# Projections that load weights for two pairs, x in four resting buffers, and causal pairs made ahead in pinned steps

## The chip, the cores and the metric

The kernel runs on one core of one Trainium2 chip. The core has a matmul engine (TensorE, PE), whose weight loads the profile lists as PEld, an elementwise engine (VectorE, DVE), an activation engine (ScalarE, ACT), GpSimd (POOL) and an engine that here only issues DMAs (SyncE, SP). Each works through its own queue in order. The metric is device time in microseconds (us) of one execution, the median of the runs; lower is better.

## The reference

The input x has the shape (4, 512, 128, 64): four batches, 512 time steps, and D = 128 x 64 = 8192 features. All is float32. Layer 0 does, for each batch:

```
xn = layernorm(x)                                  # over D
k, v, r = xn @ Wk, xn @ Wv, sigmoid(xn @ Wr)       # D -> 64
s[t] = decay * s[t-1] + k[t] * v[t]
x = x + (r * s) @ Wo                               # 64 -> D
x = x + gelu(conv3 over the 128 (layernorm(x)))    # 64 -> 64 channels
to = depthwise causal conv of 3 taps over time (layernorm(x))
x = x + layernorm(to)
x = x + gelu(x @ W1 + b1) @ W2 + b2                # 64 -> 256 -> 64
```

Layer 1 takes a moving average over 25 steps as the trend, sends the rest through a Fourier transform over time, mixes 128 modes with complex weights for each of the 64 channels, transforms back and adds the trend. The change touches layer 0 only.

## The kernel before

Layer 0 keeps features on the 128 partitions and time on the free axis: D is 64 chunks of 128, handled as 32 pairs of chunks (`NPR`), a tile of 128 x 2 x 512 values each. Each batch goes through these stages, which are Python generators:

- J, `project` (L321): for each pair it loads weights (L337, 256 KB), the transposed x (`load_x`, L293, 512 KB) and the same part of x with tokens on the partitions (`xk`, L340, 512 KB). DVE takes statistics of `xk` (L344) and scales the weights in place (L357); PE multiplies (L360). `xk` serves the statistics and nothing else.
- Z, `scan` (L371): the recurrence over time.
- A, `attend_and_convolve` (L466): the output of the attention, then the convolution over frequency. It uses the tags x1, z, x2 and sq; its result goes to DRAM as `x2d`.
- C, `convolve_time` (L581): the causal convolution over time. For a pair, `taps` (L553) loads `x2d` (L555), normalizes in two DVE operations (L556, L557), scales on ACT for each half j of the pair (L560), adds two taps per half on DVE (L564), corrects the first two time steps on POOL (L568) and stores to `tod` (L569, from POOL's queue).
- O, `open_feed` (L639), and F, `feed_forward` (L647): 64 steps c and two that drain. A step widens chunk c (`widen`, L656, into the banks m and c, gelu on ACT at L660), prepares the residual of a later pair (`residual`, L619, in even steps: loads at L549, DVE at L624 and L625; `add_residual`, L628, in odd steps: ACT at L633, DVE at L636), narrows chunk c - 1 (`narrow`, L662: PE at L667 into the single bank p, DVE empties it into x4t at L672) and transposes and stores chunk c - 2 (`store`, L675, L681 to L692).

Two stages of different batches run side by side. `in_turn` (L726) steps whichever of the two is behind by its share; this fixes the order in which instructions are traced. PE keeps that order exactly (`manual_schedule`). On the other engines, DMA queues included, a planner orders the instructions: it runs a model of the program, and whenever an engine is free in that model it takes, of the instructions whose data and buffers are ready, the one traced first. So work traced late can go early. `tc.keep_in_program_order(ins)` takes from an instruction the freedom to go ahead of the instruction traced just before it on its engine.

Around the change, F of batch 0 runs beside J and Z of batch 2, and F of batch 1 beside J and Z of batch 3. In these two stages F also works ahead: `convolve_ahead` (L571) builds the two rows that scale batch b + 1 (`rows`, L279: `spread` at L240 writes the bank p, ACT copies it at L284) and then makes `AHEAD` = 12 of the 32 pairs of the causal convolution of batch b + 1, in tiles x1 (three buffers) and z (four). `feed_forward` calls it at the head of every fourth step:

```
        for c in range(NCH + 2):
            if b + 2 < B and c % 4 == 3:
                early = early or convolve_ahead(b + 1)
                next(early, None)
```

Steps 3 and 7 make the rows, steps 11, 15, ... 55 a pair each.

In J of batches 1, 2 and 3 (once a scan is done) weights and `xk` of a pair share one tile of the tag wx, which has two buffers:

```
                both = spare("wx", 4 * S + SL)
                wq, xk = both[:, :, 0 : 4 * S], both[:, :, 4 * S :]
```

Of the kernel before, what the change touches and what calls it, by code (L numbers as in the profile page):

```python
# [12 lines left out]
ALU = mybir.AluOpType  # L13
# [9 lines left out]
SL = 512  # L23
# [3 lines left out]
S = 64  # L27
# [52 lines left out]
def layer0(ctx, tc, dram, x, xt, vecs, wkvr, wo, wdec, wconv, fbias, w1, fb1, w2, fb2, x4):  # L80
# [4 lines left out]
    nc = tc.nc  # L85
    B = x.shape[0]
# [7 lines left out]
    bk = ctx.enter_context(tc.tile_pool(name="bk", bufs=2))  # L94
# [8 lines left out]
    def two(pool, tag):  # L103
        return pool.tile([P, 2, SL], F32, tag=tag, name=tag)
# [183 lines left out]
    def pair_of(row):  # L288
        return row.unsqueeze(1).to_broadcast([P, 2, SL])

    def load_x(b, i):
        xp = fr.tile([P, 2, SL], F32, tag="xp", name="xp")
        nc.sync.dma_start(xp, xt[b, 2 * i : 2 * i + 2].rearrange("c p t -> p c t"))  # L293
        return xp

    def spare(tag, n):
        return fr.tile([P, 2, n], F32, tag=tag, name=tag, bufs={"z": 4, "wx": 2}.get(tag, 3))
# [23 lines left out]
    def project(b):  # L321
        pa = two(ps_m, "m") if b == 1 else two(ps_a, "a")
        held[0] = b == 1
        if b == 0:
            psum_w = ps_p.tile([P, SL], F32, tag="p", name="psum_w")
        stt = rowp.tile([P, NT, NS, 6], F32, tag="stt", name="stt")
        for i in range(NPR):
            first, last = i == 0, i == NPR - 1
            if unscanned[0]:

                wq, xk = two(fr, "x1")[:, :, 0 : 4 * S + 3], spare("z", SL)
            else:

                both = spare("wx", 4 * S + SL)
                wq, xk = both[:, :, 0 : 4 * S], both[:, :, 4 * S :]
            n = 4 * S + 2 * (b == 0)
            nc.sync.dma_start(wq[:, :, 0 : n], wkvr[2 * i : 2 * i + 2, :, 0 : n].rearrange("c p s -> p c s"))  # L337
            xp = load_x(b, i)
            s, h = i // 2, i % 2 * 2
            nc.sync.dma_start(  # L340
                xk, x[b, h * P : (h + 2) * P, s * SL : (s + 1) * SL].rearrange("(t p) d -> p t d", p=P)
            )
            for t in range(2):
                nc.vector.bn_stats(stt[:, h + t, s, :], xk[:, t, :])  # L344
            if b == 0:
                nc.gpsimd.memset(wq[:, :, n:], 1.0)
                for j in range(2):
                    c = 2 * i + j

                    w = wq[:, j, :]  # L350
                    nc.tensor.matmul(
                        psum_w[0 : S + 2, 0 : 4 * S + 3], lhsT=w[:, 3 * S : 4 * S + 2], rhs=w,
                        start=c == 0, stop=c == NCH - 1,
                    )
            for j in range(2):
                w = wq[:, j, 0 : 3 * S]
                nc.vector.tensor_scalar_mul(w, w, vec[:, G1, 2 * i + j : 2 * i + j + 1])  # L357
            for j in range(2):
                for k in range(2):
                    nc.tensor.matmul(  # L360
                        pa[:, k, :], lhsT=wq[:, j, k * P : (k + 1) * P], rhs=xp[:, j, :],
                        start=first and j == 0, stop=last and j == 1,
                    )
                yield 1.0
        kvrg = rowp.tile([P, 2, SL], F32, tag="kvrg", name="kvrg")
        nc.scalar.copy(kvrg, pa)
        held[0] = False
        projected[b] = (kvrg, stt, psum_w) if b == 0 else (kvrg, stt)
# [181 lines left out]
        return t  # L550


    def taps(b, i, x2, xr, to, rb, mb):  # L553

        nc.sync.dma_start(x2, x2d[b][2 * i : 2 * i + 2].rearrange("c p t -> p c t"))  # L555
        nc.vector.tensor_tensor(xr, x2, pair_of(rb), ALU.mult)  # L556
        nc.vector.tensor_tensor(xr, xr, pair_of(mb), ALU.subtract)  # L557
        for j in range(2):
            c = slice(2 * i + j, 2 * i + j + 1)
            nc.scalar.activation(  # L560
                to[:, j, :], xr[:, j, :], AF.Identity, bias=tb_all[:, c], scale=vec[:, W2, c]
            )
            for k, w in ((1, W1), (2, W0)):
                nc.vector.scalar_tensor_tensor(  # L564
                    to[:, j, k:], xr[:, j, : SL - k], vec[:, w, c], to[:, j, k:], ALU.mult, ALU.add
                )
        cc = slice(2 * i, 2 * i + 2)
        nc.gpsimd.tensor_tensor(to[:, :, 0:2], to[:, :, 0:2], fix[:, cc, :], ALU.add)  # L568
        nc.gpsimd.dma_start(tod[b][cc].rearrange("c p t -> p c t"), to)  # L569

    def convolve_ahead(b):  # L571


        rb, mb = yield from rows(of_p, *carried[b], "rm3")
        ahead[b] = rb, mb
        for i in range(AHEAD):
            xr = spare("x1", SL)
            taps(b, i, xr, xr, spare("z", SL), rb, mb)
            yield

    def convolve_time(b):  # L581
        bank = of_a if b == B - 1 else of_p
        made = AHEAD if b in ahead else 0
        moment = carried.pop(b)
        if made:
            rb, mb = ahead.pop(b)
        else:
            rb, mb = yield from rows(bank, *moment, "rm" if b == B - 1 else "rm3")
        st = bank()
        waiting, added = [], 0  # L590
        n = NPR - made
        for k in range(n + 2):
            while waiting and waiting[0][0] == k - 2:
                add_up(st, 0, *waiting.pop(0)[1:], added == 0, added == NPR - 1)
                added += 1
            if k < n:
                if b == B - 1:

                    x2, xr, to, sq = spare("xp", SL), spare("x1", SL), spare("z", SL), two(bk, "sq")
                else:  # L600
                    x2 = bk.tile([P, 2, SL], F32, tag="kx", name="x2", bufs=3)
                    xr, to = two(bk, "kd"), bk.tile([P, 2, SL], F32, tag="k3", name="to", bufs=3)
                    sq = bk.tile([P, 2, SL], F32, tag="sq4", name="sq4", bufs=2)
                taps(b, made + k, x2, xr, to, rb, mb)
                nc.scalar.activation(sq, to, AF.Square)
                waiting.append((k, to, sq))
                i = k * made // n
                if i != (k + 1) * made // n:

                    to = fetch("kh", tod, b, i)  # L610
                    sq = bk.tile([P, 2, SL], F32, tag="mid", name="sq5", bufs=4)
                    nc.scalar.activation(sq, to, AF.Square)
                    waiting.append((k, to, sq))
            yield 7.0 * (NPR + 2) / (n + 2)
        mean, sq = yield from finish(st, bank, 4)
        causal[b] = moments(mean, sq, 4)
# [30 lines left out]
    def feed_forward(b):  # L647
# [28 lines left out]
        def store(c):  # L676
            x4t = x4s.pop(c)
            pool, tag = (ps_s, "s") if free_s[0] else (ps_p, "p")
            pt = pool.tile([P, NT, P], F32, tag=tag, name="pt")
            for t in range(NT):  # L680
                nc.tensor.transpose(pt[:, t, :], x4t[:, t * P : (t + 1) * P], ident)  # L681
            s = c // 4
            if c % 4 == 0:
                obs[s] = bk.tile([P, NT, SL], F32, tag="ob", name="ob")
            o = obs[s][:, :, c % 4 * P : (c % 4 + 1) * P]
            if c // 2 % 2:
                for h in range(2):
                    nc.scalar.copy(o[:, :, halves[1 - h]], pt[:, :, halves[h]])
            else:
                nc.scalar.copy(o, pt)  # L690
            if c % 4 == 3:
                nc.gpsimd.dma_start(  # L692
                    x4[b][:, s * SL : (s + 1) * SL].rearrange("(t p) d -> p t d", p=P), obs.pop(s)
                )

        early = None
        for c in range(NCH + 2):
            if b + 2 < B and c % 4 == 3:
                early = early or convolve_ahead(b + 1)
                next(early, None)  # L700
            if c < NCH:
                widen(c, 0)
                widen(c, 1)
            i = c // 2 + 2
            if i < NPR:
                if c % 2:
                    x3s[i] = add_residual(b, i, *coming)
                else:
                    coming = residual(b, i)
            if 0 < c <= NCH:  # L710
                narrow(c - 1)
            if c > 1:
                store(c - 2)
            yield 4.5


# [358 lines left out]
```

## Time and profile before

| | us |
|---|---|
| median of 3 runs | 3857.62 (3856.37 to 3858.19) |
| the profiled execution | 3842.84, its span 3840.8 |
| PE busy | 3619.7, 94% of the span |
| DVE busy | 2692.2, 70% |
| ACT busy | 1764.0, 46% |
| POOL busy | 504.2, 13% |
| DVE waiting for weights at L357 | 167.6 in 59 waits |
| DVE waiting for x at L344 | 92.8 in 60 waits |

A line of the timeline gives the start, the duration, the engine, the source line, the operation with its output and inputs, a count where neighbours are merged, and in square brackets the idle time ahead of it and what ended that. A tile is named by its tag, so "x" stands for several. Matmuls overlap, so their durations do not add up; one float32 matmul of the source appears as two instructions. In a table by stretches each engine has its busy time and, in brackets, its count of instructions; PEclk is the granted share of TensorE's clock.

The steps of F of batch 0 begin at about 822 us and those of F of batch 1 at about 1520 us.

### The profile page before, as it was taken

What the parts mean: (1) busy time and instruction counts of PE and PEld (TensorE: products, weight loads), DVE (VectorE), ACT (ScalarE), POOL (GpSimd) and SP (SyncE); (2) the same over time, 40 slices, a digit from 0 to 9 for tenths busy, and PEclk for the clock granted to TensorE, in tenths of its full rate; (3) what the DMA queues carried; (4) which work ended last, traced back from release to release, by engine and by line L of the source; (5) the groups of instructions that cost most, each with busy time, mean ns of one, the idle gap of its engine ahead of it and who ended that gap; (6) DMA issues with size and microseconds to landing.
All of it is one profiled execution on the core that took longest, in us unless ns stands there. A gap on an engine that the chain in (4) does not pass through costs nothing. (4 is left out here: it accounts for less than half of the span.)

```text
span 3840.8 us, 44890 instructions
## 1 busy us (share of the span) xinstructions
PE 3619.7 (94%) x15945; PEld 1342.6 (35%) x15945; DVE 2692.2 (70%) x3498; ACT 1764.0 (46%) x2491; POOL 504.2 (13%) x782
## 2 busy tenths in 40 slices
PE   9999999988999999899999989999989999999999
PEld 4433322233333223333322323333322753327533
DVE  4455669968656896865689799855559267893577
ACT  0023345645556564555656578867744210142100
POOL 0000012212000121110022121100012100121001
PEclk9999999999999999999999999999999999999999
DMA  9867657777765788777568677645559468994687
GB/s 312 273 216 244 222 195 253 257 246 272 256 227 185 234 276 265 252 255 235 193 232 277 215 243 260 219 154 175 186 190 284 141 212 293 306 311 160 197 292 269
DMA packets 428599, 910.71 MB, mean 237 GB/s; under 512 B 33688, under 2 KB 84056, under 8 KB 424280
## 3 DMA queue, kind: packets, MB, share of 16 engines
q1 hardware_dynamic: 350080, 634.55, 50.3%
q0 software_dynamic: 75776, 271.62, 20.1%
q8 instruction: 127, 2.08, 0.2%
q10 hardware_dynamic: 2520, 1.67, 0.2%
q14 instruction: 96, 0.79, 0.1%
HBM read 639.21 MB, written 268.50 MB: 236 GB/s over the span
## 5 line engine op out<-in xcount | busy, mean ns | idle before, releaser
L667 PE MATMUL pa<-mid,w_sb 128*64 128x512 f32 x2048 | 503.7, 613 | 70.1 <-DVE x4t L672 69.9
L660 ACT ACTIVATE mid<-m,fb_sb 128x1024 f32<-128x1024 f32 x256 | 284.7, 1112 | 243.4 <-PE m L656 243.0
L672 DVE SCALAR_TENSOR_TENSOR x4t<-pa,fb_sb,x 128x512 f32<-128x512 f32 x252 | 187.6, 745 | 208.2 <-PE pa L667 208.2
L656 PE MATMUL m<-x,w_sb 64*128 64x512 f32 x1008 | 291.6, 651 | 1.0 <-ACT mid L660 0.7
L660 ACT ACTIVATE mid<-c,fb_sb 128x1024 f32<-128x1024 f32 x256 | 283.2, 1106 | 1.6 <-PE c L656 1.6
L667 PEld LDWEIGHTS pa<-mid,w_sb 128*64 128x64 f32 x2048 | 125.8, 137 | 417.5 <-issue 221.1
L656 PE MATMUL c<-x,w_sb 64*128 64x512 f32 x1008 | 265.6, 600 | 5.0 <-ACT mid L660 4.9
L360 PE MATMUL a<-xp,wx 128*128 128x512 f32 x512 | 245.0, 605 | 6.2 <-DVE wx L357 5.5
L943 PE MATMUL b<-xin,avg_sb 128*128 128x512 f32 x512 | 230.8, 593 | 3.1 <-DVE xin L949 3.1
L920 ACT COPY two<-a 128x512 f32<-128x512 f32 x64 | 37.5, 586 | 423.9 <-PE a L915 423.9
L523 ACT ACTIVATE sq<-x 128x1024 f32<-128x1024 f32 x128 | 135.0, 1054 | 203.0 <-DVE x L520 203.0
L949 DVE TENSOR_TENSOR xin<-b,pm 128x512 f32<-128x512 f32 x256 | 159.0, 683 | 95.5 <-PE b L946 80.5
L564 DVE SCALAR_TENSOR_TENSOR to<-kd,vec,to 128x510 f32<-128x510 f32 (+1 forms) x288 | 210.5, 743 | 17.9 <-ACT to L560 16.2
L633 ACT ACTIVATE kd<-kd,vec 128x512 f32<-128x512 f32 x256 | 193.5, 809 | 7.2 <-DVE kd L625 7.2
L250 PE MATMUL st<-x,ones 128*32 128x512 f32 x512 | 174.3, 603 | 14.0 <-DVE x L520 13.8
L825 DVE COPY xf<-b 128x256 f32<-128x256 f32 x128 | 54.3, 424 | 188.4 <-PE b L889 187.8
L681 PEld LDWEIGHTS pt<-ident,x4t 128*128 128x128 f32 x1024 | 107.9, 141 | 210.3 <-ACT mid L660 155.0
L846 DVE TENSOR_TENSOR uv<-xin 128x1024 f32<-128x1024 f32 x128 | 155.2, 1228 | 35.2 <-DMA edge<-x 14.7
L344 DVE BATCH_NORM_STATS2 stt<-wx 128x6 f32<-128x512 f32 x174 | 113.0, 685 | 93.3 <-DMA wx<-in_x 92.8
L357 DVE TENSOR_SCALAR wx<-wx,vec 128x192 f32<-128x192 f32 x174 | 48.6, 316 | 184.7 <-DMA wx<-in_wkvr 167.6
L482 PE MATMUL a<-rst,wo_sb 64*128 64x512 f32 x512 | 147.6, 650 | 32.3 <-DVE x L484 30.0
L484 DVE TENSOR_TENSOR x<-a,xp 128x1024 f32<-128x1024 f32 x128 | 156.0, 1219 | 20.9 <-PE a L482 17.6
(239 smaller groups left out, 6649.0 us busy)
## 6 DMA issues: line engine op xcount, KB each, us to landing
xp<-in_xt SPq DMA_DIRECT2D x256, 512.0 KB
xin<-x SPq DMA_DIRECT2D x128, 1024.0 KB
kh<-to SPq DMA_DIRECT2D x152, 512.0 KB
x<-x POOLq DMA_DIRECT2D x128, 512.0 KB, 4.1
kx<-x SPq DMA_DIRECT2D x128, 512.0 KB
x<-ob POOLq DMA_DIRECT2D x64, 1024.0 KB, 6.6
out<-xin POOLq DMA_DIRECT2D x64, 1024.0 KB, 7.3
x<-x SPq DMA_DIRECT2D x96, 512.0 KB
```

Of the source, the lines that this page charges most:

```text
L250: nc.tensor.matmul(st[32 * q : 32 * q + 32, :], lhsT=ones, rhs=src[:, j, :], start=first, stop=last,)
L360: nc.tensor.matmul(pa[:, k, :], lhsT=wq[:, j, k * P : (k + 1) * P], rhs=xp[:, j, :], start=first and j == 0, stop=last and j == 1,)
L484: nc.vector.tensor_tensor(x1, at, xp, ALU.add)
L564: nc.vector.scalar_tensor_tensor(to[:, j, k:], xr[:, j, : SL - k], vec[:, w, c], to[:, j, k:], ALU.mult, ALU.add)
L633: tc.keep_in_program_order(nc.scalar.activation(d[:, j, :], d[:, j, :], AF.Identity, bias=vec[:, B4, c], scale=vec[:, G4, c]))
L656: nc.tensor.matmul(pm[:, h, :], lhsT=w1_sb[hs, m * P : (m + 1) * P], rhs=x3[hs, :], start=True, stop=True)
L660: nc.scalar.activation(mid, pm, AF.Gelu_apprx_tanh, bias=fb1_sb[:, m : m + 1])
L667: nc.tensor.matmul(pa[h * H : (h + 1) * H, :], lhsT=w2_sb[:, m, :], rhs=mid[:, h, :], start=(m == 0), stop=(m == 1),)
L672: nc.vector.scalar_tensor_tensor(x4t, pa, fb2_sb, x3s[c // 2][:, c % 2, :], ALU.add, ALU.add)
L846: nc.vector.tensor_tensor(t, xin[:, 0:2, :], xin[:, 2:4, :], op)
L943: nc.tensor.matmul(po[j], lhsT=avg_sb[:, j, :], rhs=xin[:, j, :], start=True, stop=False)
L949: nc.vector.tensor_tensor(by_n(xin[:, j, :]), by_n(po[j]), by_c(pm[j % 2][:, j // 2, :]), ALU.add)
```

## The change

In `project`, batch 1 keeps the old tiles. For batches 2 and 3 the weights of two pairs (four chunks) come with one load into a wx tile, at every even pair; `xk` goes into tiles of x2 and sq in turn, two buffers each, which rest between A of one batch and A of the next. `taps` is split into `normed` (the load and the norm) and `tapped` (the rest). `convolve_ahead` yields after each half. With `pinned`, the first norm operation and the first tap of the pair's first half are kept in program order. `feed_forward` calls the generator at the end of odd steps from 9 on, instead of at the head of every fourth from 3 on: steps 9 and 11 make the rows, a pair i is normed in step 13 + 4 i and tapped in step 15 + 4 i, the last in step 59. `convolve_time` calls both halves together, unpinned.

```diff
@@ project
-            else:
+            elif b == 1:
                 both = spare("wx", 4 * S + SL)
                 wq, xk = both[:, :, 0 : 4 * S], both[:, :, 4 * S :]
-            n = 4 * S + 2 * (b == 0)
-            nc.sync.dma_start(wq[:, :, 0 : n], wkvr[2 * i : 2 * i + 2, :, 0 : n].rearrange("c p s -> p c s"))
+            else:
+                xk = two(bk, "sq" if i % 2 else "x2")
+                if i % 2 == 0:
+                    pairs = spare("wx", 4 * S + SL).rearrange("p k n -> p (k n)")[:, 0 : 16 * S]
+                    pairs = pairs.rearrange("p (c s) -> p c s", c=4)
+                    nc.sync.dma_start(pairs, wkvr[2 * i : 2 * i + 4, :, 0 : 4 * S].rearrange("c p s -> p c s"))
+                wq = pairs[:, i % 2 * 2 : i % 2 * 2 + 2, :]
+            if b < 2:
+                n = 4 * S + 2 * (b == 0)
+                nc.sync.dma_start(wq[:, :, 0 : n], wkvr[2 * i : 2 * i + 2, :, 0 : n].rearrange("c p s -> p c s"))
@@ taps, now in two
-    def taps(b, i, x2, xr, to, rb, mb):
+    def normed(b, i, x2, xr, rb, mb, pinned=False):
         nc.sync.dma_start(x2, x2d[b][2 * i : 2 * i + 2].rearrange("c p t -> p c t"))
-        nc.vector.tensor_tensor(xr, x2, pair_of(rb), ALU.mult)
+        first = nc.vector.tensor_tensor(xr, x2, pair_of(rb), ALU.mult)
+        if pinned:
+            tc.keep_in_program_order(first)
         nc.vector.tensor_tensor(xr, xr, pair_of(mb), ALU.subtract)
+
+    def tapped(b, i, xr, to, pinned=False):
         for j in range(2):
...
             for k, w in ((1, W1), (2, W0)):
-                nc.vector.scalar_tensor_tensor(
+                tap = nc.vector.scalar_tensor_tensor(
                     to[:, j, k:], xr[:, j, : SL - k], vec[:, w, c], to[:, j, k:], ALU.mult, ALU.add
                 )
+                if pinned and j == 0 and k == 1:
+                    tc.keep_in_program_order(tap)
@@ convolve_ahead
-            taps(b, i, xr, xr, spare("z", SL), rb, mb)
+            normed(b, i, xr, xr, rb, mb, True)
+            yield
+            tapped(b, i, xr, spare("z", SL), True)
             yield
@@ convolve_time
-                taps(b, made + k, x2, xr, to, rb, mb)
+                normed(b, made + k, x2, xr, rb, mb)
+                tapped(b, made + k, xr, to)
@@ feed_forward
-            if b + 2 < B and c % 4 == 3:
-                early = early or convolve_ahead(b + 1)
-                next(early, None)
...
             if c > 1:
                 store(c - 2)
+            if b + 2 < B and c > 8 and c % 2:
+                early = early or convolve_ahead(b + 1)
+                next(early, None)
             yield 4.5
```

## The prediction

> **What bounds the kernel now.** I read the page first. TensorE (PE) is busy for most of the span and VectorE (DVE) comes next, so time can only be won where PE stands.
>
> ```profile
> span 3840.8 us, 44890 instructions
> PE 3619.7 (94%) x15945; PEld 1342.6 (35%) x15945; DVE 2692.2 (70%) x3498; ACT 1764.0 (46%) x2491; POOL 504.2 (13%) x782
> ```
>
> PE's order is written by hand and the change leaves it alone but for two small groups of matmuls, so I looked at the two stages that the diff touches: the feed-forward of batch 0 beside the projection of batch 2 (822 to about 1236 us), and the same for batches 1 and 3 (1520 to 1932). The table by stretches, for PE, PEld, DVE, ACT, POOL, then granted clock, DMA share and GB/s:
>
> ```profile
> 866.00:1000.00 134.00, 112.94 (x424) 41.08 (x424) 113.89 (x150) 75.44 (x102) 24.23 (x28) 0.96 0.78 270
> 1000.00:1188.00 188.00, 184.66 (x730) 67.69 (x728) 104.74 (x140) 104.56 (x139) 7.37 (x10) 1.00 0.65 225
> 1562.00:1694.00 132.00, 112.52 (x427) 41.22 (x428) 112.51 (x149) 76.54 (x104) 22.00 (x28) 0.96 0.78 274
> 1694.00:1884.00 190.00, 189.53 (x750) 69.63 (x746) 103.84 (x142) 105.62 (x142) 7.36 (x10) 1.00 0.71 235
> ```
>
> In each stage one stretch has DVE 85% busy and PE standing for 20 us; the stretch behind it has PE at 98 to 100%. The same table for the norm of the ahead pairs (L556) has its twelve operations (14.5 us) between 820 and 988 us and none behind: all twelve pairs run in the first stretch, though the source spreads them over steps 11 to 55 of 64. The timeline of PE names what it waits for, in square brackets:
>
> ```profile
> 869.82 2.08 PE L240 MATMUL p<-ident,mrs 128*128 128x128 f32 x8 [3.03 <-DVE x4t L672]
> 896.60 3.60 PE L667 MATMUL pa<-mid,w_sb 128*64 128x512 f32 x8 [2.38 <-DVE x4t L672]
> 905.47 1.94 PE L667 MATMUL pa<-mid,w_sb 128*64 128x512 f32 x8 [1.05 <-DVE x4t L672]
> 928.07 1.94 PE L667 MATMUL pa<-mid,w_sb 128*64 128x512 f32 x8 [1.61 <-DVE x4t L672]
> 959.99 1.94 PE L667 MATMUL pa<-mid,w_sb 128*64 128x512 f32 x8 [2.64 <-DVE x4t L672]
> ```
>
> The second matmul (L667) needs the one PSUM bank that x4t (L672) empties. What DVE did before the x4t of 895.80, which released the second line, and of 869.02, which released the first:
>
> ```profile
> 889.11 3.38 DVE L564 SCALAR_TENSOR_TENSOR z<-x,vec,z 128x510 f32<-128x510 f32 x5
> 892.40 1.22 DVE L556 TENSOR_TENSOR x<-x,rm 128x1024 f32<-128x1024 f32 x1
> 894.66 1.23 DVE L556 TENSOR_TENSOR x<-x,rm 128x1024 f32<-128x1024 f32 x1 [1.04 <-DMA x<-x]
> 895.80 0.75 DVE L672 SCALAR_TENSOR_TENSOR x4t<-pa,fb_sb,x 128x512 f32<-128x512 f32 x1
> ...
> 868.56 0.55 DVE L357 TENSOR_SCALAR wx<-wx,vec 128x192 f32<-128x192 f32 x2 [5.48 <-DMA wx<-in_wkvr]
> 869.02 0.75 DVE L672 SCALAR_TENSOR_TENSOR x4t<-pa,fb_sb,x 128x512 f32<-128x512 f32 x1
> ```
>
> So there are two causes: ahead pairs packed in front of x4t, and weights whose scaling (L357) stands in DVE's queue before they have landed.
>
> **What can be won.** A step issues 8 widening instructions (L656). The first stretches hold 142 and 144 of them, 17.75 and 18 steps at 7.55 and 7.33 us; the second 246 and 248, 30.75 and 31 steps at 6.11 and 6.13. The excess is 17.75 x 1.44 = 25.5 us and 18 x 1.20 = 21.7. At the stages' starts PE waits 2.96 us (826.86) and 2.59 (1514.65) for the scaling of weights. Together **52.7 us**.
>
> A rule bears on the clock in this. The Trainium skill, "TensorE: Matmul & The Clock Gate", Part 1, has the clock fall to half after an idle window of about 3.4 us. By it only the one gap above that (3.48 us at 1565.90) costs clock, about 1.7 us. The rows differ: after a gap of only 2.38 us the L667 group of 896.60 took 3.60 us instead of 1.94, and the stretched groups at 869.82, 896.60, 1565.90, 1600.04 and 1629.66 add up to 0.9 + 1.7 + 0.9 + 1.6 + 0.9 = 6.0 us. They are inside the 52.7; by the rule it would be 48.4. I take the rows.
>
> A second rule speaks against the change. "Perfetto Trace Analysis", Identifying Performance Opportunities, reads the same gap repeating on the engine that should be saturated as a sign of too few buffers. The bank of L667 is single and stays so, and then the gaps would stay, with only the weights' waits won (2.96 + 2.59 + 3.03 + 3.48, and 1.8 of clock, 14 us: 3844). But between 1694 and 1884 the same single bank goes with PE 189.53 of 190 us busy. The bank suffices when x4t comes in time; I cost the pairs as winnable.
>
> **The change, part by part.**
>
> *Weights of two pairs per load.* Per stage 32 loads of 256 KB (L337) become 16 of 512: the same bytes, 16 x 0.42 = 7 us less of issue on SP, which is not on the path. A buffer now frees two pairs before its next use instead of one: 24 us of lead at 12 us a pair, against waits of at most 6.1 us. That covers the waits at the start and the 5.48 us, counted above. The 53.0 and 53.5 us that DVE waits for weights in the second stretches are worth nothing alone, since PE is full there; they are the room into which the pairs go. If that room stayed blocked, the pairs would fill no gap (third rival).
>
> *Token-major x in four buffers (x2, sq).* The load is no longer tied to a weights buffer, so to PE's progress: it waits only for the statistics (L344) of the pair four back. Nothing pins them, and the planner runs unpinned work as early as its data lets it, as the twelve pairs show. The 64 statistics of a stage (44 us at 0.685) and 16.8 MB of x will move towards its start. Beneath: DVE is idle there (1.77 of 12 us busy from 792 to 804), so nothing or a small gain. Above: each of four links of the DVE chain that opens the stage stands behind a statistic whose x is late, at the longest wait seen, 4.1 us: 16 us. Its usual wait is 93 us over 60, or 1.5; three links give about 4 us. I take **4 a stage, 8**.
>
> *Rows of the ahead scales* (the spread, L240, and its copy) move from the starts of steps 3 and 7 to the ends of 9 and 11. There the projection's 1.9 us no longer lies between the second matmul and the spread that needs the same bank; only the transposes do, 0.5 us. In the old place the spread waited 0.64 and 1.13 us where the weights were not late; without the cover that is 2.0 to 3.0, and x4t alone (0.75) gives no less than 0.3. **1.5 x 4 = 6**.
>
> *Twelve pairs in pinned steps.* Same operations, two steps to a piece: norm at steps 13, 17, ... 57 (2 x 1.22 us of DVE), taps at 15, ... 59 (4 x 0.743, 2 x 0.81 of ACT, the POOL fix and store). The pin puts a norm behind the x4t of its step. Queued behind it are the next L624, L625, L357 and then x4t. From one second matmul to the next lie 0.5 + 1.9 + 0.95 + 0.95 = 4.3 us, x4t takes 0.75: 3.5 of slack. DVE rises from 104.7/188, 13.6 us in four steps, to 19.0 of 24.4, or 78%. Bounds: no stall at all, or the packed stretch's 1.2 to 1.44 a step in all 46 steps, 60 a stage. The nearest rows lie between: the attention beside convolution at 1344 to 1440 us has DVE at 95% and PE losing 1.8 in 96; the feed-forward at 2400 to 2496 has DVE at 88% and loses 8.2. At 78% and pinned I take 0.6 a pair: **24 x 0.6 = 14**. The loads of x2 (L555) have three x1 buffers, over 40 us of lead. On POOL the fix (0.9) and the store (0.73) come later, behind the x4 stores; z and x1 come free at step 60, before the next attention begins behind step 63, some 4 steps of 4 us. That cover hides it; without it a few us.
>
> **Sum.** 52.7 - 8 - 6 - 14 = 24.7, say 25 us won. The profiled execution took 3842.84 us (span 3840.8 and 2.0 around it), so 3818 by it. The median of the runs is 3857.62, 15 above that execution; I take the difference over: **3833 us**.
>
> **Rivals.**
>
> *All of it comes* (0.22): slack hides the pieces and the idle start hides the statistics; only the rows' 6 is paid. 47 won: 3811. For it: PE at 99.8% with DVE idle for 86 of 190 us. Against: DVE at 78% on average is higher in its odd steps.
>
> *An exchange* (0.17): statistics, the unpinned second half's taps (j = 1) and late x fill DVE's queue in the pairs' place and the gaps move rather than vanish; about 3853, with 0 to 10 us won. For it: nothing limits the statistics; the pin binds two instructions of a pair. Not doing what it says is this case.
>
> *Slower* (0.15): the place is DVE's queue in front of x4t at steps 0 to about 30. The statistics run ahead at up to what DMA gives (359 GB/s at its best slice against 230 in use), each late x holds DVE, and the pinned norm must follow. The price is the packed 1.3 us a step. At 28 steps a stage that is 2 x 28 x 1.3 = 73, against 52.7: 20 lost, 3878. It decides from 20 packed steps a stage. Against: x alone is 16.8 MB, 130 us or 21 steps of the free 129 GB/s, just about there.
>
> **How the numbers follow.** My forecast (3833, its own range 3820 to 3846) has 0.46, the rivals 0.22, 0.17, 0.15. A measurement of this kernel tells 0.2%, 7.7 us, from nothing: 3850 to 3865 is the same. Faster: 0.46 + 0.22 + 0.03 of the exchange = 0.71. Same: 0.12. Slower: 0.15 + 0.02 = 0.17. The range leaves out the best of the first rival and most of the last: 3803 to 3867.
>
> **What would show it.** L556 spread from 900 to 1190 us at one per 24; the stretch from 866 at 6.2 us a step instead of 7.55; DVE's waits for in_wkvr down from 167.6 us to under half; x loads early in the stage with DMA near 0.9 there; waits of L240 for x4t of 1 to 2 us. I am wrong if L667 waits for x4t over 1 us a step elsewhere, most likely with L344 in front of it, or if x4t waits behind a pinned norm.

## The result, and the profile after

The changed kernel ("after" below, the other is "before") takes **3827.07 us** (median of five runs, 3821.31 to 3840.34) against 3857.62 before (median of five, 3854.13 to 3868.55). The ratio is 0.993, with a 95% interval of 0.9911 to 0.9949: 20 to 34 us faster. Run again beside the experiments it gave 3831.55 against 3859.3, a ratio of 0.9924 (0.9904 to 0.9945).

The page of the profiled execution:

```profile
span 3838.6 us, 44851 instructions
PE 3630.4 (95%) x15945; PEld 1345.7 (35%) x15945; DVE 2687.1 (70%) x3498; ACT 1761.3 (46%) x2491; POOL 507.6 (13%) x782
```

This span is only 2.2 us below that of before, and that misleads. The execution (3840.34 us) is the slowest of its five, while the profiled execution of before (3842.84) was faster than all five of its runs. A good part of the difference lies where the change does nothing. Between 480 and 552 us, for example, where the source is unchanged, the granted clock was 0.82, 0.89 and 0.78 in three stretches of 24 us, against 1.00, 0.93 and 1.00 before; after came to J of batch 2 13.4 us later than before. So I compare the two stages that the diff touches, each from the first projection matmul of J to the first attention matmul of the stage behind it:

| stage, us | before | after |
|---|---|---|
| batch 0's F beside batch 2's J | 795.3 to 1250.4: 455.1 | 808.6 to 1252.9: 444.3 |
| batch 1's F beside batch 3's J | 1493.7 to 1939.7: 446.1 | 1497.7 to 1934.2: 436.5 |
| both | 901.2 | 880.8 |

The stages became 20.4 us shorter. The table by stretches of after has the columns of the table shown of before (PE, PEld, DVE, ACT, POOL, granted clock, DMA share, GB/s):

```profile
866.00:912.00 46.00, 35.13 (x128) 13.79 (x128) 36.36 (x54) 18.49 (x25) 1.59 (x2) 0.89 0.97 342
912.00:1000.00 88.00, 87.51 (x348) 32.57 (x348) 53.53 (x76) 51.74 (x69) 8.08 (x10) 1.00 0.58 203
866.00:1000.00 134.00, 122.64 (x475) 46.36 (x476) 89.89 (x129) 70.23 (x94) 9.66 (x12) 0.96 0.71 251
1000.00:1188.00 188.00, 185.44 (x732) 68.08 (x732) 118.38 (x146) 113.11 (x153) 19.50 (x24) 1.00 0.64 227
1562.00:1694.00 132.00, 116.93 (x460) 44.77 (x460) 88.59 (x126) 66.80 (x90) 9.61 (x12) 0.96 0.71 245
1694.00:1884.00 190.00, 190.00 (x758) 70.32 (x756) 122.40 (x151) 119.27 (x160) 20.36 (x24) 1.00 0.67 229
```

From 866 to 1000 us PE is busy 9.7 us more than before and DVE 24 us less; behind 1000 us DVE has 13.6 us more and PE is as full as it was. The third line hides two states: up to 912 us PE stands idle for 11 of 46 us, with DMA at 0.97 of its time; from 912 us on it stands for half a microsecond in 88. In widening matmuls (L674 now, eight a step) the first part holds 40, so 5 steps at 9.2 us, and the second 114, so 14.25 steps at 6.18. In the first part after is even worse than before. These are the two kernels from 840 to 912 us, before and then after:

```profile
840.00:912.00 72.00, 63.98 (x240) 24.29 (x240) 53.32 (x68) 37.45 (x51) 6.62 (x10) 0.93 0.64 227
840.00:912.00 72.00, 60.27 (x222) 22.56 (x221) 57.33 (x85) 32.20 (x42) 1.59 (x2) 0.93 0.97 346
```

DVE's statistics (L353) explain the first part. Their table (DVE's busy time, count, then clock, DMA share, GB/s) has 45 of the 55 operations that run behind 820 us in the first 80 us:

```profile
820.00:900.00 80.00, 28.63 (x45) 0.96 0.94 329
900.00:1190.00 290.00, 6.48 (x10) 0.99 0.64 225
```

PE's timeline names what it waits for:

```profile
826.96 2.08 PE L240 MATMUL p<-ident,rs 128*128 128x128 f32 x8 [4.59 <-POOL rs L232]
...
868.98 1.94 PE L685 MATMUL pa<-mid,w_sb 128*64 128x512 f32 x8 [0.87 <-DVE x4t L690]
877.60 3.44 PE L685 MATMUL pa<-mid,w_sb 128*64 128x512 f32 x8 [2.46 <-DVE x4t L690]
...
907.72 2.08 PE L240 MATMUL p<-ident,rs 128*128 128x128 f32 x8 [5.17 <-DVE x4t L690]
```

In DVE's timeline, this stands ahead of the x4t that released the last of these lines:

```profile
903.62 1.29 DVE L353 BATCH_NORM_STATS2 stt<-x 128x6 f32<-128x512 f32 x2 [2.46 <-DMA x<-in_x]
904.98 1.29 DVE L353 BATCH_NORM_STATS2 stt<-sq 128x6 f32<-128x512 f32 x2
906.32 0.69 DVE L353 BATCH_NORM_STATS2 stt<-x 128x6 f32<-128x512 f32 x1
906.93 0.73 DVE L690 SCALAR_TENSOR_TENSOR x4t<-pa,fb_sb,x 128x512 f32<-128x512 f32 x1
```

A statistic whose x is late stands there, and four more behind it, all ahead of the x4t for which PE waits. No wait of PE between 840 and 912 us ended on a transfer itself; the busy DMA engines held up PE only through DVE. The ahead pairs have become nearly harmless, and the statistics have taken a part of their place. In before all twelve norms had run by 988 us; in after the table of the norms (L565) shows about one for each 24 us behind 900 us:

```profile
820.00:900.00 80.00, 0.00 (x0) 0.96 0.94 329
900.00:1000.00 100.00, 3.64 (x3) 0.97 0.62 220
1000.00:1100.00 100.00, 4.85 (x4) 1.00 0.66 232
1100.00:1200.00 100.00, 4.86 (x4) 1.00 0.63 221
```

### The profile page after: what moved, and what is told of

Its sections match the earlier page's. It is cut to its first block, busy times and chain, and to the rows that moved or that the text cites. A ratio compares the mean times of both kernels' runs of the same rounds, so it can differ in the third digit from the quotient of the medians.

```text
span 3838.6 us, 44851 instructions
## 1 busy us (share of the span) xinstructions
PE 3630.4 (95%) x15945; PEld 1345.7 (35%) x15945; DVE 2687.1 (70%) x3498; ACT 1761.3 (46%) x2491; POOL 507.6 (13%) x782
## 5 line engine op out<-in xcount | busy, mean ns | idle before, releaser
L685 PE MATMUL pa<-mid,w_sb 128*64 128x512 f32 x2048 | 501.1, 610 | 57.7 <-DVE x4t L690 57.1
L674 PE MATMUL m<-x,w_sb 64*128 64x512 f32 x1008 | 289.8, 647 | 0.0
L685 PEld LDWEIGHTS pa<-mid,w_sb 128*64 128x64 f32 x2048 | 125.3, 136 | 402.0 <-issue 246.0
L674 PE MATMUL c<-x,w_sb 64*128 64x512 f32 x1008 | 263.5, 596 | 1.3 <-ACT mid L678 1.3
L250 PE MATMUL st<-x,ones 128*32 128x512 f32 x512 | 172.6, 605 | 13.9 <-DVE x L529 13.7
L699 PE MATMUL pt<-ident,x4t 128*128 128x128 f32 x1024 | 169.3, 288 | 1.5 <-ACT ob L706 1.5
L530 POOL DMA_DIRECT2D x<-x x128 | 93.3, 729 | 575.8 <-DVE x L529 545.8
```

The source lines that it names most:

```text
L250: nc.tensor.matmul(st[32 * q : 32 * q + 32, :], lhsT=ones, rhs=src[:, j, :], start=first, stop=last,)
L674: nc.tensor.matmul(pm[:, h, :], lhsT=w1_sb[hs, m * P : (m + 1) * P], rhs=x3[hs, :], start=True, stop=True)
L685: nc.tensor.matmul(pa[h * H : (h + 1) * H, :], lhsT=w2_sb[:, m, :], rhs=mid[:, h, :], start=(m == 0), stop=(m == 1),)
```

## The experiments

All compute the whole reference. Ratios are to the kernel before on the same chip. "Stages" is the sum of the two stages as above, in the one profiled execution; before is 901.2.

**Each half alone.** e1 is before with the change's `project` only:

```diff
-            else:
+            elif b == 1:
...
+                xk = two(bk, "sq" if i % 2 else "x2")
...
+                    nc.sync.dma_start(pairs, wkvr[2 * i : 2 * i + 4, :, 0 : 4 * S].rearrange("c p s -> p c s"))
```

> Only the projection is changed (weights of two pairs per load, x in four resting buffers); the ahead pairs are made as before, at steps 3 to 55 and unpinned. In the planned order of VectorE the statistics of x then stand at steps 0 to 18 and the twelve pairs at 6 to 19, so the packed stretch stays. Theory (the pairs' packing in front of x4t is what costs, and x that is free of the weights adds to it): 3850 to 3875, no faster than before. Rival one (late weights were the cost, and the early load is the gain): near the changed kernel, 3825 to 3835, with the waits for weights below half.

e2 is the other half: the change with the `project` of before.

```diff
-            taps(b, i, xr, xr, spare("z", SL), rb, mb)
+            normed(b, i, xr, xr, rb, mb, True)
+            yield
+            tapped(b, i, xr, spare("z", SL), True)
...
+            if b + 2 < B and c > 8 and c % 2:
```

> Only the ahead pairs are changed (pinned steps 13 to 59); the projection loads weights and x of one pair into one tile as before. Theory: the pinned steps carry nearly all of the gain, and without x running ahead the stages open without DMA at its limit: 3815 to 3838. Rival one (late weights block VectorE for 53 us in each second stretch, so pieces put there stall PE unless the weights come early): 3845 to 3865, with PE waiting for x4t by 0.5 us or more in most steps from 13 on.

Measured: e1 3861.7 against 3861.72, ratio 0.9998 (0.9986 to 1.0011), stages 907.2. e2 3853.57, ratio 0.9979 (0.9969 to 0.9988), stages 901.5. Alone they give nothing and 8 us, together 27 to 31; for e2 I had expected 3815 to 3838. So weights and x in the new buffers are worth nothing by themselves. The pinned pieces are worth more with them, though e9 below shows another way to the same gain. In e2, DVE's and PE's waits between 920 and 1160 us (engine, line, what it waited for, us in total, times, longest) show why:

```profile
DVE wx L357 <- DMA wx<-in_wkvr: 26.2, 10, 3.8
...
DVE stt L344 <- DMA wx<-in_x: 13.3, 10, 2.0
...
PE pa L676 <- DVE x4t L681: 12.3, 8, 2.4
```

The pieces are spread, but the tied weights and x are each late ten times. DVE waits 39.5 us for them, with x4t queued behind, and PE waits 1.3 to 2.4 us once in about 26 us, the four steps of an ahead pair. In the second stage it is worse: from 1640 to 1880 us DVE waits 58.0 us for weights in 11 waits, up to 7.5 us long, and PE 18.8 us for x4t in 10.

**The pins.** e3 is the whole change without them:

```diff
-            normed(b, i, xr, xr, rb, mb, True)
+            normed(b, i, xr, xr, rb, mb)
             yield
-            tapped(b, i, xr, spare("z", SL), True)
+            tapped(b, i, xr, spare("z", SL))
```

> The whole change, but without the two pins of a pair; the places in the source are those of the change. In the planned order the norms then stand at steps 9 to 21 instead of 13 to 57. Theory (the pins do it): the packed stretch is back, and longer by the statistics of x ahead of it: 3850 to 3880. Rival two (the later place at the ends of odd steps does it, pins or not): 3825 to 3835.

Measured: 3862.64, ratio 1.0005 (0.9994 to 1.0016), stages 912.0. The norms run early again, all before 1000 us:

```profile
820.00:1000.00 180.00, 14.65 (x12) 0.95 0.84 286
1000.00:1190.00 190.00, 0.00 (x0) 0.98 0.53 185
```

The new places in the source do nothing by themselves; the pins do the work. Both pins went at once here, so which of the two is needed is open.

**The statistics.** e4 pins them too:

```diff
-                nc.vector.bn_stats(stt[:, h + t, s, :], xk[:, t, :])
+                stat = nc.vector.bn_stats(stt[:, h + t, s, :], xk[:, t, :])
+                if b > 1:
+                    tc.keep_in_program_order(stat)
```

> The whole change, and the statistics of x of batches 2 and 3 are kept in program order too, so that two stand in every second step up to 52 instead of all 64 in steps 0 to 9. Theory (x running ahead is what PE still loses at the start of each of the two stages, some 20 us each between the first projection matmul and the rows): the losses there fall by half or more, 3800 to 3818, and DMA from 850 to 910 us falls from 1.0 to about 0.7. Rival three (VectorE and DMA have room there, and the starts lose the time to the chain that opens the stage): 3824 to 3832, no change.

e5 is the change unaltered, for comparison:

> The changed kernel once more, unaltered, beside the three that follow and on their chip. Expected by the first comparison (ratio 0.993): 3827 to 3840 where the kernel before takes 3862, and the two stages, from the first projection matmul to the first attention matmul of the next stage, 435 to 446 us each.

Measured: e4 3812.14, ratio 0.9861 (0.9836 to 0.9886), stages 852.0. e5 3831.55, ratio 0.9924, stages 879.6. The pin takes 28.8 us from the stages of after; by the ratios it is 0.63%, 24 us. In e4 14 statistics run between 820 and 900 us, instead of 45, and 44 between 900 and 1190. The table by stretches of e4:

```profile
840.00:912.00 72.00, 67.87 (x264) 24.71 (x263) 40.68 (x57) 38.56 (x50) 1.59 (x2) 0.98 0.70 237
912.00:1000.00 88.00, 87.58 (x348) 32.44 (x344) 60.88 (x79) 50.90 (x69) 7.63 (x9) 0.99 0.76 261
1000.00:1188.00 188.00, 185.32 (x746) 69.63 (x744) 140.27 (x185) 115.92 (x158) 20.98 (x25) 1.00 0.73 253
```

After had PE busy 60.27 of the 72 us in the first of these. A part of what is left in e4 is late weights, as in these two lines of its DVE timeline:

```profile
908.23 0.55 DVE L368 TENSOR_SCALAR wx<-wx,vec 128x192 f32<-128x192 f32 x2 [8.09 <-DMA wx<-in_wkvr]
908.70 0.75 DVE L692 SCALAR_TENSOR_TENSOR x4t<-pa,fb_sb,x 128x512 f32<-128x512 f32 x1
```

**Pinned statistics without pinned pieces.** e8 is e4 with the edit of e3. I had come to think that PE loses in proportion to what is packed early, so that either pin would win its own share (3836 to 3844).

> Statistics pinned, pieces not: the planned norms stand at steps 9 to 22. It separates what the pairs' packing costs when x does not run ahead. Theory (the two packings add up): 20 to 27 us per two stages better than without any pin, which was 3862, so 3836 to 3844. Rival (any packing of 20 steps costs the same, the rest is hidden behind it): 3855 to 3862.

Measured: 3856.31, ratio 0.9994 (0.9982 to 1.0006), stages 902.9. The shares do not add. Pinning the pieces alone won 0.8%, and 1.3% beside pinned statistics; pinning the statistics alone nothing. Without pins DVE ran the statistics first and the norms behind them (e3); here the norms fill its queue as before:

```profile
820.00:1000.00 180.00, 14.57 (x12) 0.98 0.78 266
1000.00:1190.00 190.00, 0.00 (x0) 0.97 0.63 213
```

In e8's table by stretches, DVE is busy for 82.63 of 88 us and PE stands for 15.5 of them, and behind 1000 us for another 11.6 of 188:

```profile
912.00:1000.00 88.00, 72.48 (x274) 25.38 (x272) 82.63 (x110) 51.96 (x72) 19.24 (x24) 0.98 0.85 292
1000.00:1188.00 188.00, 176.44 (x677) 64.73 (x679) 101.70 (x132) 98.34 (x130) 6.77 (x9) 0.97 0.63 213
```

What e8 gains on e3 from 840 to 912 us (PE 68.15 us of 72, against 59.36) it loses in part behind, where e3 has PE at 75.98 and 178.18 us. Why freeing both kinds of work costs no more than freeing the pieces alone stays open.

**Weights: how many, and where they are scaled.** e6 is e4 with one pair for each load:

```diff
-                if i % 2 == 0:
-                    pairs = spare("wx", 4 * S + SL).rearrange("p k n -> p (k n)")[:, 0 : 16 * S]
...
+                wq = spare("wx", 4 * S + SL)[:, :, 0 : 4 * S]
+                nc.sync.dma_start(wq, wkvr[2 * i : 2 * i + 2, :, 0 : 4 * S].rearrange("c p s -> p c s"))
```

> As the version with the statistics pinned, but weights of one pair per load; x stays in its four resting buffers. The planned order of VectorE then has the scaling of a pair one step ahead of its matmuls, as against one to five. Theory (what the version with pinned pieces alone lacked, 8 us won where the whole change wins 27, is weights that land in time): back to 3840 to 3855, VectorE's waits for in_wkvr at 40 us or more in the first stage. Rival (it lacked an x that is free of the weights tile, and the size of the load does nothing): 3808 to 3820 as with two pairs.

e7 keeps the two pairs of e4 but scales a pair's weights one pair ahead of its matmuls, pinned there. Its `weights(i)`, left out here, makes the load of pairs i and i + 1:

```diff
...
+    def scale_by_g(wq, i, pinned):
+        for j in range(2):
+            w = wq[:, j, 0 : 3 * S]
+            mul = nc.vector.tensor_scalar_mul(w, w, vec[:, G1, 2 * i + j : 2 * i + j + 1])
+            if pinned:
+                tc.keep_in_program_order(mul)
...
+                if i == 0:
+                    coming = weights(0)
+                    scale_by_g(coming[0], 0, False)
+                wq = coming[i]
...
+            if b < 2:
+                scale_by_g(wq, i, False)
+            elif i + 1 < NPR:
+                if (i + 1) % 2 == 0:
+                    coming.update(weights(i + 1))
+                scale_by_g(coming[i + 1], i + 1, True)
```

> As the version with the statistics pinned, and the scaling of a pair's weights is traced one pair ahead and kept in program order, so that it stands two steps ahead of its matmuls throughout and not up to five. Theory (a scaling that is planned before its weights have landed is the last thing that holds x4t; the version with pinned statistics still shows waits of 5.7 and 8.1 us for it, with 1.6 and 2.3 us of PE behind them, at the start of each stage): 3800 to 3808, with no wait for x4t over 1 us from 840 us on. Rival (weights of the first pairs are late by DMA, wherever the scaling stands): 3810 to 3818.

Measured: e6 3821.54, ratio 0.9908 (0.9886 to 0.9929), stages 867.5. e7 **3791.69**, ratio 0.9824 (0.9803 to 0.9846), stages 834.0: the best of all, 68 us below before and below the 3800 to 3808 that I had expected. The intervals of e4 and e6 touch (0.9886), so a gain by the load of two pairs, 0.47% as measured, is not clear of noise. Those of e4 and e7 overlap a little; e10 below settles it. In e6 DVE waits for weights 46.0 us in 15 waits between 844 and 1190 us, in e4 24.4 in 10, in e7 only this:

```profile
DVE wx L330 <- DMA wx<-in_wkvr: 3.3, 1, 3.3
```

And PE fills the first stage, with all pieces and statistics in it:

```profile
840.00:912.00 72.00, 71.47 (x287) 27.00 (x285) 44.21 (x57) 39.22 (x52) 1.59 (x2) 1.00 0.73 257
912.00:1000.00 88.00, 88.00 (x351) 32.23 (x348) 63.24 (x83) 54.00 (x74) 8.40 (x10) 1.00 0.75 263
1000.00:1188.00 188.00, 188.00 (x761) 70.50 (x759) 140.15 (x190) 118.05 (x161) 21.17 (x26) 1.00 0.73 257
```

**Are the buffers needed at all?** e9 pins the statistics on e2, so weights and x of a pair share a tile as before. It is e2 with the edit of e4.

> As the version with the pinned pieces alone (weights and x of one pair in one tile, as before), and the statistics of x kept in program order. The version with pieces alone won 8 us, the one with one pair of weights per load, x resting and statistics pinned won 35. They differ in the tile of x and in the pin of its statistics. Theory (x in the weights' tile is what costs: its load and its statistics hold the tile, so the next weights come later): 3848 to 3858, as without the pin. Rival (the place of the statistics is what costs): 3818 to 3832, as with x resting.

e10 is e7 with one pair for each load (its `weights(i)` loads pair i alone):

```diff
-                if (i + 1) % 2 == 0:
-                    coming.update(weights(i + 1))
+                coming.update(weights(i + 1))
```

> As the version with statistics pinned and scaling one pair ahead, but weights of one pair per load. Theory (the load of two pairs gives the lead that the scaling needs; with one pair and two buffers a load can start only when the pair before it is done, one pair ahead of use, and lands 5 to 8 us later): 3805 to 3830, with waits for in_wkvr at 30 us or more in each stage. Rival (the place of the scaling does it, whatever the load): 3788 to 3800.

Measured: e9 3814.96 against 3857.73, ratio 0.9882 (0.986 to 0.9903), stages 858.7. e10 3798.56, ratio 0.9837 (0.9817 to 0.9858), stages 839.5. Both of my theories fell. The tied tile with pinned statistics is as good as e4 within the intervals. One pair for each load, scaled ahead, comes within 0.13% of e7, and the intervals overlap. The step from e6 to e10, with one pair in both, shows the worth of the scaling ahead clear of noise (0.9908 to 0.9837). In e9 the pin holds back no packing: in e2 and in e9 alike 14 statistics run from 820 to 900 us and 42 from 900 to 1190. It changes what stands beside x4t within the steps. In e9, between 920 and 1160 us, DVE waits for weights nearly as in e2, but no longer for x:

```profile
DVE x4t L683 <- PE pa L678: 40.8, 18, 4.1
DVE wx L359 <- DMA wx<-in_wkvr: 23.5, 9, 3.7
```

In e10 DVE waits for no transfer at all in that stretch. What it waits for longest is PE, so x4t is ready to follow PE and not the other way round:

```profile
DVE x4t L705 <- PE pa L700: 59.3, 29, 3.7
```

## Why the prediction was right, and where its sum was not

Faster was the likeliest case, and the time is 6 us below the 3833 forecast. The main mechanism was right: packed pairs in front of x4t, which the pins spread (e3). That the number came so close is in good part luck, for the sum (24.7 us, against 20.4 in the stages) comes from errors that cancel. The runs give each term, in us of both stages:

| term of the prediction | predicted | measured | from |
|---|---|---|---|
| what can be won | 52.7 | 67.1 | before - e7 |
| left to late weights | 0 | 17.9 | e4 - e7 |
| statistics early (8) and rows (6) | 14 | 28.8 | after - e4 |
| pinned pieces | 14 | 0 to 2 | e7, after |
| won | 24.7 | 20.4 | before - after |

The measured rows join up by construction, but for the pieces, whose cost lies within the others. They hold for this order of the steps (after, e4, e7); since the shares do not add (e8), another order could give others. Single executions carry some us of their own: in all eleven profiled executions the stages compare 1 to 9 us worse with before than the ratios do, so the profiled stages of before were probably some 5 us short. That covers a good part of what lies between 20.4 and the 27 to 31 of the medians; what remains is within the interval. Outside the two stages the span varied from 2940 to 2964 us between executions.

**What can be won** was too low, since I took the second stretches, PE 98 to 100% busy, for the floor. Between 1000 and 1188 us e7 has 256 widening matmuls, 32 steps at 5.88 us, where before had 6.11. PE's order of work is the same there, and the ends of matmuls in the profile are modelled, so probably short waits hide inside a busy PE: before has 730 PE instructions in 184.66 busy us there, e7 761 in 188.00.

**Weights of two pairs**: PE's waits of 2.96 and 2.59 us at the stages' starts went, as forecast. But the step that 24 us of lead cover waits of at most 6.1 us failed. DVE's waits for weights fell from 167.6 us to 107.2 over the kernel, not to under half, and e4 still has one of 8.09 in front of x4t. e10 cures it with one pair for each load: the depth of the load was not the question, but when DVE's queue reaches the scaling. That they are worth nothing alone was right (e1).

**Token-major x in four buffers**: the mechanism was right, statistics and loads at the stage's start, DMA at 0.94 to 1.0. The size was the term that failed. I priced only the chain that opens the stage, at 4 us for each. PE's wait for it grew by 2.5 us in the first stage (4.59 at 826.96, 2.09 before) and showed no wait in the second; the cost came behind it, where the statistics stood in front of x4t until 912 us. My rival "slower" had this place and this mechanism; it decides from 20 packed steps, and up to 912 us there were 10 (80 widening matmuls): from 840 to 912 us PE stood 11.7 us, against 4.1 in e4. From 866 to 912 us after made 5 steps where e4 made 7, and in 1562 to 1694 us 18.75 where e4 made 20.75: four steps of 6 us, most of the 28.8.

**Rows**: in after the four waits of L240 for x4t are 5.17, 0.27, 6.85 and 1.44 us, 13.7 in all, where I had 6 and named 1 to 2 each. In e4 the three waits that are left sum to 0.8. So my lower bound (0.3 each) was the price of the move, and the rest came from the statistics: this edit was priced too high and that of x too low.

**Pinned pieces**: 0.6 a pair was too much. Between 1000 and 1188 us PE waits for x4t twice in after (1.12 and 1.17 us), each time behind weights that were late by about 2.5 us and not behind a norm, and 1694 to 1884 us has PE at 190.00 of 190 with DVE at 64%. In e7 DVE is at 75% and PE still full. I had priced them by the feed-forward at 2400 us, where DVE is at 88% and nothing on it is pinned: the wrong row. The 3.5 us of slack that I worked out were the better guide.

**The two rules.** For the clock the rows were right and the 3.4 us of the Trainium skill's "TensorE: Matmul & The Clock Gate" (Part 1) too long: after the gap of 2.46 us at 877.60 in after the L685 group took 3.44 us instead of 1.94, and the granted clock was 0.86 in the 12 us around it. But the length of the gap does not decide alone: 2.49 us at 1575.95 in after left the group at 1.94, and 1.89 at 1600.04 in before stretched it to 3.53. The reading of equal gaps as too few buffers, which "Perfetto Trace Analysis", Identifying Performance Opportunities, gives as a possible one, did not hold here: e7 has the same single bank, and between 840 and 1190 us no wait of PE for x4t over 0.27 us.

**What stays open.** The second stage of e2 (454.1) is longer than that of before (446.1), while its first is shorter (447.4). Its trace shows later weights ahead of x4t there, but not why they are later. Not tried were the old tied tile with the scaling ahead, which e9 and e10 suggest to be near e7, and a scaling that is pinned in its old place: e7 both moves and pins it.

## What to carry to other kernels

Where an engine works its queue in order, ask of every entry that needs a transfer when the transfer lands, and put the entry behind the work that others wait for, until then; here this was worth more (e4 and e7, another 40 us) than the buffers that the change added (e1, nothing). Freeing a load from the resource that held it back frees the work on it too, and a planner that takes whatever its model has ready can put that work in front of work that others wait for (after, 45 statistics in the first 80 us). Before you price a stall by the share of busy time of another stage, look at whether the order in that stage is fixed in the same way.

## What was not expected of the hardware

With x loads unbound, the DMA engines of after were busy in whole stretches of 12 us (share 1.02 to 1.04) at 368 to 371 GB/s. That is no new height: the prediction's 359 is found in one stretch of 12 us in before (1620 to 1632), and from 1588 to 1600 us before moved 380. New is how long it lasts, 346 GB/s from 840 to 912 us against 227.

Between 480 and 552 us the granted clock differed by up to 0.22 between the profiled executions of before and after, though the source of what runs there is unchanged. It is not a trait of the kernel: e5, the same program in another execution, had 0.99, 0.87 and 0.99 in the three stretches. So a stage must be compared by itself.
